# Layer 0 of a graph network: the products that place a quad's sums come two steps behind the sums, in two persistent PSUM tiles

## The chip, the cores and the metric

The kernel runs on one core of one Trainium2 chip. The metric is the device time of one execution in microseconds (us); less is better. The engines are TensorE (PE; PEld is its weight load), VectorE (DVE), ScalarE (ACT), GpSimd (POOL) and SyncE (SP), each with its own queue of instructions that it works off in order. PE can write only to PSUM, and DVE and ACT fetch its results from there.

## What is computed

Two layers over a graph of 3125 nodes with 128 features each and 100000 edges, which are sorted by their target node `dst`.

```python
# layer 0
summed = segment_sum(x[src], dst); deg = segment_sum(1, dst)
x = layernorm(x + elu((summed / maximum(deg, 1)) @ W + b))
# layer 1: attention per relation (4 relations, 4 heads of 128)
xl = einsum('nf,rfh->nrh', x, W_l); xr = einsum('nf,rfh->nrh', x, W_r)
z = leaky_relu(xl[src, type] + xr[dst, type] + e_feat)
score = einsum('ehc,ehc->eh', z, att[type]); alpha = softmax per (dst, type)
h_msg = gated mean over heads of segment_sum(alpha * xl[src, type])
h1 = layernorm(x + h_msg); h2 = layernorm(h1 + silu(h1 @ Wf1) @ Wf2)
x = layernorm(x + h2)
```

The change is in layer 0. Its sum over the edges of a node is what the steps below work out; while they run, the kernel also makes the tables xl and xr of layer 1 and turns the edges' attributes.

## The kernel before

The edges lie in 784 tiles of 128, four of which make a quad: 196 quads. The sums of layer 0 for all nodes are gathered in one accumulator in SBUF, acc0, that holds for each node 128 sums and its degree (repeated). The first 72 quads are handled by counting (`count`: for a block of nodes a matrix of counts is made and multiplied with the rows of x). The other 124 quads, u = 72 to 195, go through gathered rows, one quad in each step of a loop:

- `gather` (L768): POOL fetches the rows x[src] of a tile of 128 edges by an indirect DMA into a ring of 24 tiles, xg.
- `onehot4` (L1116): DVE makes for each of the quad's four tiles a one-hot matrix, edge by one of 32 neighbouring nodes.
- `sums0` (L1148): PE multiplies, so that the 32 sums of each tile come out, in the four quarters of a PSUM tile sg of 128 partitions x 129 columns (128 features and the count). After each of the four products the gather for the tile 24 further on is issued.
- `out_copy` (L1158): ACT copies sg to SBUF, sgs.
- `spread0` (L1162): DVE makes one more one-hot matrix, ohq, that says at which of 64 nodes each of the 4 x 32 sums belongs.
- `out0` (L1166): PE first makes six products whose result is used by nothing (il x ic, 300 columns of bf16 each, into columns 128 and up of the PSUM tile fo; called dummies below), and then the two products that place the quad's sums at their nodes, into columns 0 to 127 of fo.
- `add0` (L1176): DVE adds fo to acc0, at a column that it reads from a register.

All engines are handed their instructions through `Ordered` (L637), which keeps for each engine the order in which the program issues them; so the loop over the steps (L1360 to L1402) writes out by hand the order of every queue. The framework places the waits between the engines by the tiles that instructions read and write. PSUM has eight banks and all are in use: the pool l0p has one buffer each for mp, sg, fo and dn, the pool m0p one for mw and three for xp. l0 is a pool in SBUF, with two buffers of each tile where nothing else is said.

In step s the quad is u = 72 + s, and the order is: loads and stores on SP that are due; `out_copy(u-1)`; in steps that have edge work (each 2.3 steps or so), four transposes on PE of the edge attributes with ACT's copy emt (`turned`); halves of the table xr (DVE); `onehot4(u+1)` and `spread0(u)`; `out0(u-1)`; the edge work's products (`lin`); the counting matrices with `add0(u-1)` behind the first or instead of them; small jobs of a block; `sums0(u)`; a burst of products for the tables xl and xr of a block (`tables`, with ACT's copies xlr); and the stores of the edge work (`keep`: one of lb_d and four of eat_d on SP).

A block is 128 nodes whose sums are complete. `block(b, s)` (L1263) puts its phases into the steps from s on: it takes the sums, divides, multiplies with W, applies elu and layernorm, turns the result, and makes the block's part of the tables. L1352 says when it starts: when the last quad that has an edge to the block is behind (`behind`, L658), or at fixed steps for the first four.

```python
if u < NQ:
    spread0(u)
...
if UD < u <= NQ:
    out0(u - 1)
```

UD is 72 and NQ is 196.

Of the kernel before, what the change touches and what calls it, by code (L numbers as in the profile page):

```python
# [9 lines left out]
F32 = mybir.dt.float32  # L10
# [10 lines left out]
P = 128  # L21
N = 3125
E = 100000
F = 128
R = 4
H = 4
HC = H * F
# [594 lines left out]
WQ = 64  # L622
# [5 lines left out]
NQ = TT // 4  # L628
# [29 lines left out]
def behind(b):  # L658

    return min(NQ, -(-int(TT * (P * (b + 1) / N) ** 0.5 + 6) // 4))  # L660
# [5 lines left out]
UD, ND, SHI = 72, 240, NB2  # L666
# [26 lines left out]
def windows(ctx: ExitStack, tc: tile.TileContext, a, out, flag):  # L693
# [44 lines left out]
    def node(t, eng):  # L738
        return nc.values_load(d0_i[0:1, t:t + 1], engines=[eng], min_val=0, max_val=N - 1,
                              skip_runtime_bounds_check_because="a node's number")  # L740
# [16 lines left out]
    with tc.tile_pool(name="l0c", bufs=1) as l0c:  # L757
# [6 lines left out]
        ic = l0c.tile([P, 16 * SHI], BF16, name="ic")  # L764
        il = l0c.tile([P, P], BF16, name="il")
        pool = Ordered(tc, nc.gpsimd)

        def gather(t):  # L768
            pool.indirect_dma_start(out=xg[:, t % XG, :F], out_offset=None, in_=a["x"], in_offset=of_tile(t, src_e))


        with tc.tile_pool(name="pr", bufs=1) as pr, tc.tile_pool(name="prp", bufs=2, space=PSUM) as prp:
# [95 lines left out]
            b, k, f, l = (rm[:, :, o:o + P] for o in (0, P + 2, 2 * P + 2, 3 * P + 2))  # L868
# [15 lines left out]
        with tc.tile_pool(name="m0c", bufs=1) as m0c, tc.tile_pool(name="l0", bufs=2) as l0, \  # L884
# [3 lines left out]
            pe, ve, act, sp = (Ordered(tc, e) for e in (nc.tensor, nc.vector, nc.scalar, nc.sync))  # L888
# [224 lines left out]

            X = {}

            def onehot4(u):  # L1116
                o = X["oh", u] = l0.tile([P, 4, WA], F32, name="oh", bufs=3)
                ve.tensor_tensor(o, loc_e[:, 4 * u:4 * u + 4].unsqueeze(2).to_broadcast([P, 4, WA]),
                                 iw[:, :WA].unsqueeze(1).to_broadcast([P, 4, WA]), op=OP.is_equal)

            def turned(us):
                mp = bank()
                for j, u in enumerate(us):
                    c, i0 = u // QC, u * 4 % TR
                    pe.transpose(mp[:, j], ees[c][:, i0:i0 + 4].rearrange("p t s d -> p (t s d)"), ident)
                em = l0.tile([P, 4, P], F32R, name="emt", bufs=2)
                act.activation(em, mp, AF.Copy)
                X["emt", us[0]] = em

            def lin(us):  # L1130
                em = X["emt", us[0]].bitcast(F32)
                ln = X["ln"] = m0p.tile([P, 4, 4, H * R], F32, name="mw")
                for j in range(4):
                    pe.matmul(ln[:, j], em[:, j], vt, start=True, stop=True)

            def lin_add(us):
                lb = X["lb"] = l0.tile([P, 16, H, R], F32, name="lb")
                tng = others(4 * us[0])
                ve.tensor_tensor(lb, X.pop("ln").rearrange("p j t (h r) -> p (j t) h r", r=R),
                                 tng.unsqueeze(2).to_broadcast([P, 16, H, R]), op=OP.add)  # L1140

            def keep(us):
                sp.dma_start(lb_d[us[0] // 4], X.pop("lb").rearrange("p t h r -> p (t h r)"))
                em = X.pop(("emt", us[0])).bitcast(F32)
                for j, u in enumerate(us):
                    sp.dma_start(eat_d[u].rearrange("x (t e) -> t x e", t=4), em[:, j])

            def sums0(u):  # L1148
                o = X.pop(("oh", u))
                sg = l0p.tile([P, F + 1], F32, name="sg")  # L1150
                for i in range(4):
                    t = 4 * u + i
                    pe.matmul(sg[i * WA:(i + 1) * WA], o[:, i], xg[:, t % XG], start=True, stop=True)
                    if t + XG < TT:
                        gather(t + XG)
                X["sg", u] = sg

            def out_copy(u):  # L1158
                g = X["sgs", u] = l0.tile([P, F + 1], F32, name="sgs")
                act.activation(g, X.pop(("sg", u)), AF.Copy)  # L1160

            def spread0(u):  # L1162
                q = X["ohq", u] = l0.tile([P, WQ], F32, name="ohq")
                ve.tensor_scalar(q, iw[:, :WQ], rv[:, u:u + 1], None, op0=OP.is_equal)

            def out0(u):  # L1166
                g, q = X.pop(("sgs", u)), X.pop(("ohq", u))

                fb_ = l0p.tile([P, HC], F32, name="fo")
                for _ in range(6):  # L1170
                    pe.matmul(fb_[:, 2 * WQ:2 * WQ + 12 * SHI], il, ic[:, :12 * SHI], start=True, stop=True)
                fo = X["fo", u] = fb_[:, :2 * WQ].rearrange("p (a b) -> p a b", a=2)
                pe.matmul(fo[:, 0], g[:, :F], q, start=True, stop=True)
                pe.matmul(fo[:, 1], g[:, F:].to_broadcast([P, P]), q, start=True, stop=True)

            def add0(u):  # L1176
                n = node(4 * u, ENG.DVE)
                ve.tensor_tensor(acc0[:, :, ds(n, WQ)], acc0[:, :, ds(n, WQ)], X.pop(("fo", u)), op=OP.add)
# [18 lines left out]
            def count(u):  # L1197
                w = counted(u)
                cn = l0p.tile([P, SHI, w], F32, name="dn")
                for i in range(4):  # L1200
                    t = 4 * u + i
                    ol = l0.tile([P, P], BF16, name="ol", bufs=4)
                    ve.tensor_scalar(ol, il, lo_f[:, t:t + 1], None, op0=OP.is_equal)
                    oc = l0.tile([P, SHI * w], BF16, name="oc", bufs=4)
                    ve.tensor_scalar(oc, ic[:, :SHI * w], c_f[:, t:t + 1], None, op0=OP.is_equal)
                    pe.matmul(cn.rearrange("p a b -> p (a b)"), ol, oc, start=(i == 0), stop=(i == 3))
                X["cn", u] = cn

            def count_add(u):
                n = nc.values_load(dc_i[0:1, u:u + 1], engines=[ENG.DVE], min_val=0, max_val=ND - 1,  # L1210
                                   skip_runtime_bounds_check_because="a node's number, bounded")
                v = A[:, :, ds(n, counted(u))]
                ve.tensor_tensor(v, v, X.pop(("cn", u)), op=OP.add)
# [32 lines left out]
            C0, C2 = 3, []  # L1246
# [102 lines left out]
                    at_step(s + k[7] + 1, "half", lambda r=r: half(r))  # L1349

            for b in range(NB2):
                block(b, max(behind(b) - UD, C2[0] if b == 0 else C2[1] + 4 * (b - 1) if b < 4 else 0))  # L1352


            at_step(NS, "ve", rows_of_sources)
            for f in range(NQ // 4):
                at_step(turned_at(f), "edges", range(4 * f, 4 * f + 4))
            last = max(s for s, _ in jobs)
            onehot4(UD)
            for s in range(last + 1):  # L1360
                u = UD + s
                for f in jobs.pop((s, "sp"), []):
                    f()
                if UD < u <= NQ:
                    out_copy(u - 1)
                edges = jobs.pop((s, "edges"), [])
                for us in edges:
                    turned(us)
                halves_ = jobs.pop((s, "half"), [])
                if halves_:  # L1370
                    halves_.pop(0)()
                if u + 1 < NQ:
                    onehot4(u + 1)
                if halves_:
                    halves_.pop(0)()
                if u < NQ:
                    spread0(u)
                for f in halves_:
                    f()
                if UD < u <= NQ:  # L1380
                    out0(u - 1)
                for us in edges:
                    lin(us)
                counts = jobs.pop((s, "count"), [])
                for i, v in enumerate(counts):
                    count(v)
                    if i == 0 and UD < u <= NQ:
                        add0(u - 1)
                    count_add(v)
                if UD < u <= NQ and not counts:  # L1390
                    add0(u - 1)
                for us in edges:
                    lin_add(us)
                for e in ("act", "ve"):
                    for f in jobs.pop((s, e), []):
                        f()
                if u < NQ:
                    sums0(u)
                for f in jobs.pop((s, "burst"), []):
                    f()  # L1400
                for us in edges:
                    keep(us)  # L1402
# [5 lines left out]
    with tc.tile_pool(name="ac", bufs=1) as ac, tc.tile_pool(name="at", bufs=2) as at, \  # L1408
# [138 lines left out]
        pe, ve, act, pool, sp = (Ordered(tc, e) for e in (nc.tensor, nc.vector, nc.scalar, nc.gpsimd, nc.sync))  # L1547
# [270 lines left out]
        for s in range(-2, NQ + LATE + 2):  # L1818
            u = s - 1
# [37 lines left out]
    with tc.tile_pool(name="fc", bufs=1) as fc, tc.tile_pool(name="fw", bufs=3) as fw, \  # L1857
# [89 lines left out]
        for bs_ in QS:  # L1947
# [7 lines left out]
            b = bs_[0]  # L1955
# [28 lines left out]
```

## Time and profile before

| what | us |
|---|---|
| median of 5 runs | 2865.19 |
| lowest and highest of the 5 | 2854.01, 2869.36 |
| profiled execution | 2869.47 |
| its span, first to last instruction | 2867.6 |
| mean granted clock of TensorE over the span | 0.899 |
| layer 0's steps, in the span | 34.5 to 1077 |
| layer 1's loop, in the span | 1126 to 2786 |

The profile is of one execution. Times in a timeline count from the span's start. A row of a group gives engine, operation, out<-in with partitions x elements, and how many; behind the bar the busy time, the mean duration in ns, and the engine's idle time just ahead of these instructions with what ended it. In a timeline the bracket at a row's end is that idle time and its releaser. "remote" and "issue" are releases that the profile can't lay to an instruction of this core's engines. All of the helper's instructions have line L647, so one goes by the tiles' names. The granted clock is a share of full speed.

### The profile page before, as it was taken

How to read it: one execution, taken by the hardware profiler on the slowest of the kernel's cores; microseconds unless marked ns; L12 is line 12 of the kernel's file. 1: busy time of each engine (PE TensorE's matmuls, PEld its weight loads, DVE VectorE, ACT ScalarE, POOL GpSimd, SP SyncE). 2: the span in 40 equal slices, each digit the busy share in tenths (PEclk: the TensorE clock that was granted, in tenths of full speed). 3: DMA queues.
4: the chain of work that ended last, by engine and by line, in shares of the span. 5: the costliest groups of instructions: out<-in, count | busy, mean ns of one | idle time of the engine just before them, and what ended most of it. 6: DMA issues, size and time to landing. Idle time of an engine off the chain costs nothing.

```text
span 2867.6 us, 66163 instructions
## 1 busy us (share of the span) xinstructions
PE 2415.8 (84%) x24485; PEld 1859.7 (65%) x24485; DVE 1823.0 (64%) x6395; ACT 909.8 (32%) x1964; POOL 1245.2 (43%) x1294
## 2 busy tenths in 40 slices
PE   3677777877787785699999999999999999999964
PEld 2444454445444443477777777888888888888853
DVE  6655635653554345377777777777777777767656
ACT  0111112112222221244444444444444444333314
POOL 6544454344444413244444444444444444444400
PEclk9757778778788787799999999999999999999977
DMA  4323344334455456466666667777777789999920
GB/s 128 90 67 102 116 126 151 133 123 155 130 197 181 150 190 227 137 201 204 207 205 207 205 203 216 235 235 236 233 233 237 233 241 256 254 251 248 241 55 24
DMA packets 284394, 520.64 MB, mean 182 GB/s; under 512 B 45833, under 2 KB 144820, under 8 KB 283151
## 3 DMA queue, kind: packets, MB, share of 16 engines
q1 hardware_dynamic: 201588, 273.76, 30.6%
q0 software_dynamic: 78592, 239.71, 29.0%
q8 instruction: 194, 3.18, 0.5%
q10 hardware_dynamic: 3880, 2.84, 0.4%
q14 instruction: 140, 1.15, 0.1%
HBM read 412.10 MB, written 104.82 MB: 180 GB/s over the span
## 4 chain that ended last, share of the span: by engine, by line
PE 48%; DVE 8%; issue 3%; DMA 1%; ACT 0%; SPq 0%; DVEq 0%; ACTq 0%
PE z L647 30%; PE ag L647 7%; PE row L647 6%; DVE wo L647 4%; PE e L647 2%; PE sm_p L647 2%; DVE f L647 1%; DMA win<-xr_d 0%; DVE ea L647 0%; DVE oh L647 0%; PE f L1930 0%; PE f L1922 0%; DVE acc L647 0%; DVE y L647 0%; DMA xr_d<-xh 0%
## 5 line engine op out<-in xcount | busy, mean ns | idle before, releaser
L647 POOL DMA_INDIRECT xl<-xl_d,src_e x784 | 752.0, 959 | 890.0 <-PE ag L647 399.5
L647 POOL DMA_INDIRECT xg<-in_x_dram,src_e x496 | 488.7, 985 | 542.8 <-PE sg L647 366.3
L647 ACT ACTIVATE relu<-z 128x512 f32<-128x512 f32 x784 | 449.6, 597 | 796.3 <-PE z L647 619.5
L647 PE MATMUL z<-f_ident,xl 128*128 128x128 f32 x3136 | 476.5, 275 | 0.0
L647 PEld LDWEIGHTS z<-f_ident,xl 128*128 128x128 f32 x3136 | 369.0, 141 | 44.5 <-issue 0.8
L647 PE MATMUL z<-ea,weh 128*128 128x512 f32 x784 | 361.3, 461 | 18.1 <-issue 13.4
L647 PE MATMUL z<-oht,win 96*128 96x128 f32 (+2 forms) x1600 | 342.4, 297 | 2.2 <-DMA win<-xr_d 1.9
L647 PEld LDWEIGHTS z<-oht,win 128*128 128x128 f32 (+1 forms) x1600 | 275.3, 190 | 57.6 <-DMA win<-xr_d 2.1
L647 PE MATMUL z<-ea,wel 128*128 128x512 f32 x784 | 310.6, 396 | 0.0
L647 PE MATMUL row<-relu,attw 128*32 128x128 f32 x6272 | 246.6, 276 | 33.8 <-issue 31.2
L647 PE MATMUL ag<-xl,wo 128*32 128x128 f32 x6272 | 225.5, 278 | 7.5 <-DVE acc L647 4.2
L647 PEld LDWEIGHTS row<-relu,attw 128*32 128x32 f32 x6272 | 171.9, 109 | 88.6 <-issue 87.7
L647 DVE TENSOR_TENSOR acc<-acc,fo 128x128 f32 x124 | 35.4, 285 | 248.6 <-PE fo L647 76.5
L647 PEld LDWEIGHTS ag<-xl,wo 128*32 128x32 f32 x6272 | 180.7, 112 | 9.1 <-DVE acc L647 5.1
L647 DVE TENSOR_TENSOR_SCAN m<-rm,row 128x128 f32<-128x128 bf16 x98 | 41.3, 421 | 227.5 <-PE row L647 227.5
L647 PE MATMUL xp<-cbl,two 128*128 128x512 f32 x200 | 164.0, 820 | 24.4 <-DVE xh L647 12.7
L647 PE MATMUL fo<-ic,il 128*128 128x300 bf16 x744 | 154.0, 358 | 33.9 <-DVE acc L647 18.4
L647 PEld LDWEIGHTS z<-ea,weh 128*128 128x128 f32 x784 | 149.8, 191 | 27.4 <-issue 27.3
L647 DVE CAST xh<-xp 128x512 fp32r<-128x512 f32 x100 | 69.1, 691 | 145.7 <-PE xp L647 108.2
L647 PE MATMUL fo<-ohq,sgs 128*128 128x64 f32 x496 | 95.6, 329 | 73.3 <-issue 47.1
L647 PEld LDWEIGHTS z<-ea,wel 128*128 128x128 f32 x784 | 150.2, 192 | 8.6
L647 DVE SCALAR_TENSOR_TENSOR ea<-far,e 128x512 fp32r<-128x512 bf16 x196 | 132.3, 675 | 36.9 <-PE e L647 35.9
(327 smaller groups left out, 4034.1 us busy)
## 6 DMA issues: line engine op xcount, KB each, us to landing
win<-xr_d SPq DMA_DIRECT2D x224, 256.0 KB
xr_d<-xh SPq DMA_DIRECT2D x100, 512.0 KB
win<-xr_d SPq DMA_DIRECT2D x176, 192.0 KB
xl_d<-xlr SPq DMA_DIRECT2D x100, 258.0 KB
sg<-seg_d SPq DMA_DIRECT2D x196, 128.0 KB
rm<-rq_d SPq DMA_DIRECT2D x98, 128.5 KB
eat_d<-emt SPq DMA_DIRECT2D x196, 64.0 KB
xl<-xl_d,src_e POOLq DMA_INDIRECT x784
```

Of the source, the lines that this page charges most:

```text
L647: ins = f(*args, **kw)
```

## The change

Two PSUM tiles are made once, ahead of the loop, instead of a new tile each step: sgp with two halves of 129 columns, and fop with four parts of 128 columns. `sums0(u)` writes half u % 2 of sgp. `out0` is called for u-2 instead of u-1 and writes part u % 2 of fop; its dummies are seven of 256 columns, into parts 2 and 3 of fop, instead of six of 300. `add0` is called for u-2, too. sgs has three buffers instead of two, and ohq four instead of two. The blocks start one step later where their start depends on `behind` (from the fifth block on), so there are 129 steps instead of 128. `out_copy(u-1)`, `onehot4(u+1)`, `spread0(u)` and `sums0(u)` stay in their steps.

```diff
+            sgp = l0p.tile([P, 2, F + 1], F32, name="sg")
+            fop = l0p.tile([P, 4, P], F32, name="fo")
...
             def sums0(u):
                 o = X.pop(("oh", u))
-                sg = l0p.tile([P, F + 1], F32, name="sg")
+                sg = sgp[:, u % 2]
...
             def out_copy(u):
-                g = X["sgs", u] = l0.tile([P, F + 1], F32, name="sgs")
+                g = X["sgs", u] = l0.tile([P, F + 1], F32, name="sgs", bufs=3)
...
-                q = X["ohq", u] = l0.tile([P, WQ], F32, name="ohq")
+                q = X["ohq", u] = l0.tile([P, WQ], F32, name="ohq", bufs=4)
...
-                fb_ = l0p.tile([P, HC], F32, name="fo")
-                for _ in range(6):
-                    pe.matmul(fb_[:, 2 * WQ:2 * WQ + 12 * SHI], il, ic[:, :12 * SHI], start=True, stop=True)
-                fo = X["fo", u] = fb_[:, :2 * WQ].rearrange("p (a b) -> p a b", a=2)
+                for _ in range(7):
+                    pe.matmul(fop[:, 2:].rearrange("p a b -> p (a b)"), il, ic[:, :2 * P], start=True, stop=True)
+                fo = X["fo", u] = fop[:, u % 2].rearrange("p (a b) -> p a b", a=2)
...
-                block(b, max(behind(b) - UD, C2[0] if b == 0 else C2[1] + 4 * (b - 1) if b < 4 else 0))
+                block(b, max(behind(b) - UD + 1, C2[0] if b == 0 else C2[1] + 4 * (b - 1) if b < 4 else 0))
...
-                if UD < u <= NQ:
-                    out0(u - 1)
+                if UD + 1 < u <= NQ + 1:
+                    out0(u - 2)
...
-                    if i == 0 and UD < u <= NQ:
-                        add0(u - 1)
+                    if i == 0 and UD + 1 < u <= NQ + 1:
+                        add0(u - 2)
...
-                if UD < u <= NQ and not counts:
-                    add0(u - 1)
+                if UD + 1 < u <= NQ + 1 and not counts:
+                    add0(u - 2)
```

## Prediction

> **What bounds the kernel now.** I read the busy tenths first. TensorE is full for most of the second half, but in the first part, layer 0, it is not, and its clock changes.
>
> ```profile
> PE   3677777877787785699999999999999999999964
> PEclk9757778778788787799999999999999999999977
> ```
>
> Each digit is a slice of 71.7 us. The change touches slices 2 to 15 alone. The view of stretches, for the steps of layer 0 (34.5 to 1077 us; columns: stretch, length, busy time of PE, PEld, DVE, ACT, POOL, granted clock, DMA share, GB/s):
>
> ```profile
> 34.50:1077.00 1042.50, 787.81 (x4069) 495.13 (x4069) 522.55 (x1745) 214.70 (x509) 471.29 (x485) 0.80 0.42 136
> ```
>
> No engine is full: PE 76%, DVE 50%, POOL 45%, ACT 21%, DMA 42%. 124 steps in 1042.5 us are 8.4 us a step, so the stage is bound by hand-overs in the fixed order of issue; what is worth time is PE's idle time that nothing else would refill. The costliest groups give the stop that the change aims at:
>
> ```profile
> L647 PE MATMUL fo<-ic,il 128*128 128x300 bf16 x744 | 154.0, 358 | 33.9 <-DVE acc L647 18.4
> L647 PE MATMUL fo<-ohq,sgs 128*128 128x64 f32 x496 | 95.6, 329 | 73.3 <-issue 47.1
> ```
>
> PE stood still for 73.3 us just ahead of the placing products: that is the most that the lag can win by itself. Most of it is ended by "issue", which says nothing, so I read the timeline. PE's sums of quad 179 and what follows (columns: start, length, engine, operation, idle before and its releaser):
>
> ```profile
> 941.70 0.43 PE L647 MATMUL sg<-xg,oh 128*32 128x129 f32 x8
> ...
> 942.05 0.94 PE L647 MATMUL fo<-ic,il 128*128 128x300 bf16 x6
> ...
> 948.64 0.28 ACT L647 ACTIVATE sgs<-sg 128x129 f32<-128x129 f32 x1 [6.78 <-remote]
> ...
> 948.98 1.12 PE L647 MATMUL fo<-ohq,sgs 128*128 128x64 f32 x4 [5.98 <-issue]
> 949.78 0.55 PEld L647 LDWEIGHTS mw<-w,me 128*128 128x128 f32 x2
> 949.88 0.74 PE L647 MATMUL mw<-w,me 128*128 128x128 f32 x2
> ...
> 951.07 0.66 PE L647 MATMUL sg<-xg,oh 128*32 128x129 f32 x8
> ```
>
> The sums ended at 942.13, ACT copied them only at 948.64, and PE's placing products came 0.06 us after the copy's end (948.92). The releaser of ACT is not shown ("remote"); the copy was late, not slow (0.28 us).
>
> **The change, part by part.**
>
> *1. The placing products come from the quad before.* out0 now works on u-2, whose copy was issued a step earlier, so its stop at the copy goes. Through the timeline I sorted the 124 steps by the gap ahead of the placing products:
> - 81 steps have none: the six dummies take 0.94 us and the copy ends about 0.4 to 0.5 us after the sums. Gain 0; the dummies hide the copy.
> - 19 have a gap of 0.35 us or less, together 3.8 us, mostly 0.21 us after a burst of table products, whose copies stand ahead of this one on ACT. Gain 3.8.
> - 24 have more: 29.7 us in 10 "clear" steps, in which nothing else stops PE before the next sums, and 39.7 us in 14 "blocked" ones.
>
> Then I asked what is late next. sums0(u) writes the tile that out_copy(u-1) reads, as before. The new tile has two halves of 129 columns (1032 bytes per partition in all), and the halves would free PE entirely only if each had its own guard. The trace has one tile that several engines share by parts, hm, with four parts of 128 columns:
>
> ```profile
> 2786.24 2.82 PE L1902 MATMUL hm<-f_ident,acc 128*128 128x128 f32 x12 [0.32 <-DVE acc L647]
> 2787.40 0.50 DVE L1886 BATCH_NORM_STATS2 fst<-hm 128x6 f32<-128x128 f32 x2 [1.21 <-PE hm L1902]
> ...
> 2790.90 1.58 ACT L1905 ACTIVATE fr<-hm 128x512 f32<-128x512 f32 x3 [5.71 <-DVE fmv L1887]
> ```
>
> DVE read the first part only after the fourth was written (the first transpose of a tile ended at 2786.72, the fourth at 2787.36), and ACT's read waited until DVE's reads were over. So I take such a tile to be guarded whole: sums0(u) still waits for out_copy(u-1), and PE wins in a clear step only the work between the placing products and the next sums. Behind that stop stand, on PE, the sums, a burst of tables and the next dummies, and on POOL the gathers for quad u+6, which are issued behind the sums; all of them stood behind the old stop too. For quad 179 that is 951.07 - 948.98 = 2.09 of 5.98 us. Summed over the ten clear steps, the smaller of gap and such work is 15.2 us (quad 75: 2.46 of 5.48; 73: 1.79 of 4.05; 159: 1.05 of 6.27; 179: 2.09; 149: 1.86; 142: 1.61; 117: 1.56; 154: 1.37; 100: 0.83; 99: 0.61).
>
> The Trainium skill, "PSUM — Partial Sum Buffer", section "PSUM bank collisions raise a hardware error ⚠️", says the same from the other side: PSUM is to be guarded by bank and quadrant, not by address, because two engines in one bank collide even on different columns. By that rule the two halves of a 2 KiB bank buy no overlap between PE's sums and ACT's copy, and this part is worth the sum just given; without it the sum would be that of rival B.
>
> *Blocked steps.* There the next product needs another late thing. Quad 164:
>
> ```profile
> 809.14 1.11 PE L647 MATMUL fo<-ohq,sgs 128*128 128x64 f32 x4 [4.08 <-issue]
> ...
> 812.29 0.60 ACT L647 ACTIVATE emt<-mp 128x512 fp32r<-128x512 f32 x1 [3.19 <-remote]
> ...
> 812.94 1.97 PE L647 MATMUL mw<-vt,emt 128*128 128x64 f32 x8 [2.68 <-issue]
> ```
>
> If PE places 4.08 us earlier, it stops for ACT's emt at the same 812.94. In twelve of the fourteen the next stop is such a one (ACT's emt, or DVE's ol and oc ahead of the counts): gain 0. In two (184 and 188) a transpose can start early, so that ACT's ht and what hangs on it follow; I take 2.2 + 1.8 = 4.0 us.
>
> *2. The dummies.* Seven products of 256 columns are 1792 columns instead of 1800. Six take 0.94 us in the rows above, so seven at 256 cost about the same; they still wait for DVE's add of the step before (the wait behind 18.4 us of the row above), since they write the tile that it reads. 124 more pairs of weight load and product: 0, with 0 to 5 us as bounds (0.04 us each, if the load were not hidden).
>
> *3. More buffers* (sgs 3, ohq 4): no instruction, no DMA. add0, onehot4 and spread0 keep their places; add0 in step u adds what out0 made in the same step, as before. 0. In the stage DVE is idle for some 247 us ahead of the adds, some 75 of it for these products, but they come earlier only where PE does, so it is not counted again.
>
> *4. Blocks start a step later, and the steps are 129.* From the schedule I counted which jobs fall into the same step: table bursts with edge steps 10, then 7; halves with edges 8, then 7; means with edges 8, then 9; bursts with two-count steps 1, then 3. All DMAs of a block (its input rows, ht, xl and xr tables) move one step on SP with it; SP and the queues move 136 GB/s here and layer 1 moves over 200 in the same profile, so I give this 0, with -8 to +12 us as bounds: about one step either way.
>
> At the end, quad 195 was placed between 1075.68 and 1077.3 (dummies, 0.93; placing, 0.55; add, 0.29). Now the last step has one more round of dummies and placing behind an add, while the earlier rounds move ahead of the last burst: +0.5 to +2.5; I take +1.5.
>
> **Sum:** -3.8 - 15.2 - 4.0 + 1.5 = -21.5. The profiled execution took 2869.5 us (span 2867.6), so 2848 for a like one. It is 4.3 above the median of the runs shown, 2865.2; against that I forecast **2844**.
>
> **The rivals.**
>
> *B, the halves are guarded each by itself.* Then the clear steps win their whole 29.7 us, the small ones 3.8, and the dummies lose the 18.4 us wait for DVE's add: -52, 2813. For it: the code asks for halves. Against it: the rows of hm. 0.1.
>
> *C, nothing is won.* ACT's copy is late for a cause outside the stop. In long gaps SP is busy storing eat_d, and all of ACT, DVE and POOL show "remote" releases, as at 808.81 and 812.29. If such a delay strikes the work after the sums just as well, the 15.2 and 4.0 us come back as stops of PE ahead of sums0 or lin, and only the 3.8 is left: 2861. For it: twelve of fourteen blocked steps refill their gap already. Against it: the ten clear ones do not. Within 0.3% either way. 0.25.
>
> *D, slower, by the clock.* PE's busy time in the stage is 787.8 us at a granted clock of 0.80, and slices of it stand between 0.5 and 0.8. Whoever moves idle time from one place to another moves the stretches at a lower clock too. If the stage came out at 0.78 instead of 0.80, its busy time would be 787.8 x 0.80/0.78 = 808: +20, and if no stop of the 15.2 us is won with it, the time is 2865 + 20 - 3.8 = 2881. It decides from a loss of 0.02 on, where it eats the whole gain. For it: a PE that waits before the sums instead of between dummies and placing has its dummies, which are there to keep it busy, in another place. Against it: total idle falls. With it goes a bad placing of the shifted blocks (+12). 0.2.
>
> **How the numbers follow.** Forecast 0.45, B 0.1, C 0.25, D 0.2. About 0.3% (8.6 us) is what a measurement of this kernel can tell from no change. Faster: all of the forecast and B make 0.55. Same: C, 0.25. Slower: D, 0.2. The forecast's own range, with the 0 to 5 of the dummies and -8 to +12 of the shift, is 2836 to 2861. The range for 8 in 10 takes in C, the greater part of B's side and the lower part of D's: 2815 to 2878.
>
> **What would show it.** In the profile after: the idle ahead of the placing products falls from 73.3 us to under 10; the idle ahead of sg<-xg,oh rises by about 30 to 50, ended by ACT's sgs (if B holds, it does not, and PE does the sums of one quad while ACT copies the other); the dummies' wait for DVE's acc stays near 18; ACT's sgs rows keep their long "remote" waits; the stage ends some 20 us earlier, about 1056, at a clock of 0.80 or a little above. A stage clock below 0.79 means D. A stage as long as before, with the idle time only moved ahead of sg, means C. Layer 1 must stay as it is: if its length of 1660 us (1126 to 2786) moves by over 5 us, I have missed something.

## The result, and the profile after

The changed kernel is slower: 2883.56 us (median of 52 runs, 2867.48 to 2906.81) against 2869.21 us for the kernel before (94 runs, 2854.01 to 2893.91). The ratio is 1.0044, 95% interval 1.0033 to 1.0055, that is +12.6 us (+9.5 to +15.8) of 2869.2. Forecast was 2844, -21 us.

The profiled execution took 2870.9 us (span 2869.2) and is one of the faster ones of this kernel, so the two profiles lie only 1.5 us apart; the loss has to be read by stages and from the experiments. First the page's tenths, then the view of stretches for layer 0's steps (same columns as before), which now end at 1088 instead of 1077:

```profile
PE   2686766778787785599999999999999999999964
PEclk9667777887788787799999999999999999999977
```

```profile
34.50:1088.00 1053.50, 778.25 (x4193) 505.40 (x4193) 526.60 (x1749) 212.27 (x507) 472.96 (x485) 0.77 0.41 135
```

The steps take 11 us longer although PE is busy for 9.6 us less: PE's idle time grew. The groups of that stretch show where it went (columns: busy time, mean ns | idle time just ahead, its releasers):

```profile
L647 PE MATMUL fo<-ic,il 128*128 128x256 bf16 x868 | 153.0, 332 | 33.6 <-DVE acc L647 25.0 <-issue 8.4
L647 PE MATMUL fo<-ohq,sgs 128*128 128x64 f32 x496 | 84.8, 304 | 0.0
L647 PE MATMUL mw<-vt,emt 128*128 128x64 f32 x392 | 69.3, 335 | 61.1 <-issue 35.8 <-ACT emt L647 25.3
L647 PE MATMUL sg<-xg,oh 128*32 128x129 f32 x992 | 67.2, 353 | 28.5 <-issue 16.5 <-DVE oh L647 9.5 <-ACT sgs L647 2.5
```

The stop ahead of the placing products is gone, all 73.3 us of it. In the kernel before, the same view gives for the other two groups:

```profile
L647 PE MATMUL mw<-vt,emt 128*128 128x64 f32 x392 | 71.0, 341 | 25.8 <-issue 21.5 <-ACT emt L647 4.2
L647 PE MATMUL sg<-xg,oh 128*32 128x129 f32 x992 | 66.8, 351 | 9.3 <-DMA xf<-in_L_gnn_W_e_dram 9.3
```

So 35 us came back ahead of the edge work's products, which wait for ACT's emt, and 19 ahead of the sums; the counting products took 20 more (their idle time with that of their weight loads went from 37.8 to 57.3 us in the union of PE's records). PE's whole idle time from the first sums to the last placing, from that union of products and weight loads, is 273.5 us instead of 253.3.

One place of the changed kernel's timeline shows how (some of POOL's gathers are left in):

```profile
784.79 0.66 PE L647 MATMUL sg<-xg,oh 128*32 128x129 f32 x8
...
785.38 1.12 PE L647 MATMUL mp<-f_ident,ee 128*128 128x128 f32 x4
...
786.07 0.95 POOL L647 DMA_INDIRECT xg<-in_x_dram,src_e  x1 [0.30 <-issue]
...
786.29 1.70 PE L647 MATMUL fo<-ic,il 128*128 128x256 bf16 x7
...
787.32 0.95 POOL L647 DMA_INDIRECT xg<-in_x_dram,src_e  x1 [0.30 <-issue]
...
787.78 0.80 PE L647 MATMUL fo<-ohq,sgs 128*128 128x64 f32 x4
788.58 0.95 POOL L647 DMA_INDIRECT xg<-in_x_dram,src_e  x1 [0.30 <-issue]
790.01 0.28 ACT L647 ACTIVATE sgs<-sg 128x129 f32<-128x129 f32 x1 [6.50 <-PE fo L647]
790.18 0.94 POOL L647 DMA_INDIRECT xg<-in_x_dram,src_e  x1 [0.66 <-PE fo L647]
792.76 0.60 ACT L647 ACTIVATE emt<-mp 128x512 fp32r<-128x512 f32 x1 [2.48 <-remote]
792.88 0.29 DVE L647 TENSOR_TENSOR acc<-acc,fo 128x128 f32 x1 [5.85 <-remote]
...
793.41 1.97 PE L647 MATMUL mw<-vt,emt 128*128 128x64 f32 x8 [4.83 <-ACT emt L647]
```

PE ended the sums at 785.45, the transposes at 786.50 and the placing products at 788.58. ACT could copy the sums only at 790.01 (4.56 us late), the transposes at 792.76, and DVE could add only at 792.88 (4.30 us late), each with nothing else to do (that the first of these rows names PE's fo is the view's guess at which of PE's signals came; the copy needs the sums). PE did not stop ahead of fo, as meant, and stood at the next thing that needs ACT. All the while POOL issued one gather after the other.

### The profile page after: what moved, and what is told of

Read it like the earlier page. It is cut to its first block, busy times and chain, and to the rows that moved or that the text cites. A ratio compares the mean times of both kernels' runs of the same rounds, so it can differ in the third digit from the quotient of the medians.

```text
span 2869.2 us, 66382 instructions
## 1 busy us (share of the span) xinstructions
PE 2402.6 (84%) x24609; PEld 1866.1 (65%) x24609; DVE 1826.2 (64%) x6395; ACT 906.1 (32%) x1962; POOL 1247.0 (43%) x1294
## 4 chain that ended last, share of the span: by engine, by line
PE 48%; DVE 8%; issue 3%; DMA 1%; ACT 0%; SPq 0%; DVEq 0%; ACTq 0%
PE z L647 30%; PE ag L647 7%; PE row L647 6%; DVE wo L647 4%; PE e L647 2%; PE sm_p L647 2%; DVE f L647 0%; DMA win<-xr_d 0%; DVE ea L647 0%; DVE oh L647 0%; PE f L1932 0%; PE f L1924 0%; DVE acc L647 0%; DMA xr_d<-xh 0%; DVE fst L1888 0%
## 5 line engine op out<-in xcount | busy, mean ns | idle before, releaser
L647 DVE TENSOR_TENSOR_SCAN m<-rm,row 128x128 f32<-128x128 bf16 x98 | 41.2, 421 | 222.6 <-PE row L647 220.3
L647 PE MATMUL fo<-ic,il 128*128 128x256 bf16 x868 | 153.0, 332 | 33.6 <-DVE acc L647 25.0
L647 PE MATMUL xp<-cbl,two 128*128 128x512 f32 x200 | 167.6, 838 | 15.8 <-DVE xh L647 6.8
L647 ACT ACTIVATE xlr<-xp 128x512 f32<-128x512 f32 x100 | 59.7, 597 | 306.1 <-PE xp L647 163.1
```

The lines of the kernel that those rows point to most:

```text
L647: ins = f(*args, **kw)
```

## The experiments

Each ratio is to the kernel before, run on the same chip in the same set; the kernel's own medians differ by 1% between sets (2865.7 to 2895.8), so times are compared within a set. Ratios shift a little between sets, too: e7 and n7 are the same kernel and gave 0.9108 and 0.9080.

| run | what | ratio to before, 95% interval |
|---|---|---|
| e1_shift | blocks one step later, nothing else | 1.0041 (1.0023 to 1.0059) |
| e2_tiles | persistent tiles, 7 dummies, no lag, no shift | 1.0000 (0.9981 to 1.0018) |
| e3_lag_old_tiles | lag and shift, old tiles | 1.0052 (1.0025 to 1.0080) |
| e4_lag_no_shift | lag and tiles, blocks as before | 0.9986 (0.9964 to 1.0008) |
| e5_shift_to_19 | blocks 4 to 19 later | 1.0055 (1.0030 to 1.0081) |
| e6_shift_from_20 | blocks 20 to 24 later | 1.0028 (1.0008 to 1.0049) |
| e7_before_no_refill | no gathers in the steps | 0.9108 (0.9075 to 0.9141) |
| e8_lag_no_refill | lag, no gathers | 0.9098 (0.9062 to 0.9133) |
| e9_two_xp | two xp (yardstick) | 1.0192 (1.0157 to 1.0227) |
| e10_lag_two_banks | lag, two banks for sg, two xp | 1.0216 (1.0178 to 1.0253) |
| e11_plain_loads | SP's plain loads for the gathers | 0.9193 (0.9157 to 0.9228) |
| e13_edges_too | blocks 1 to 24 and edge work later | 1.0074 (1.0045 to 1.0104) |
| n7_no_refill | as e7, yardstick | 0.9080 (0.9043 to 0.9117) |
| n1_shift_no_refill | shift, no gathers | 0.9120 (0.9079 to 0.9162) |
| n5_to_19_no_refill | blocks 4 to 19 later, no gathers | 0.9114 (0.9076 to 0.9153) |
| n6_from_20_no_refill | blocks 20 to 24 later, no gathers | 0.9071 (0.9034 to 0.9108) |
| n14_all_later_no_refill | all 25 blocks later, no gathers | 0.9128 (0.9097 to 0.9159) |
| m1_lag_all_later | the change, with blocks 0 to 3 later too | 1.0016 (0.9997 to 1.0035) |

**Which part of the change costs.** Three theories: the later blocks, the dummies and tiles, or the lag itself. Four kernels take the parts singly.

```diff
 e1:  block(b, max(behind(b) - UD + 1, ...))            on the kernel before
 e2:  sgp, fop and 7 dummies of 256                     on the kernel before
 e3:  sg, fo and 6 dummies of 300 as before             on the changed kernel
 e4:  block(b, max(behind(b) - UD, ...))                on the changed kernel
```

> The kernel before with nothing but the blocks' start one step later (from the fifth block on, 129 steps). If the loss of 12 to 14 us is the later blocks (their last phases end one step of about 8.4 us later, and their jobs fall on other edge steps), this alone gives +8 to +14 us. If the lag or the dummies make the loss, it is within 4 us of the kernel before.

> The kernel before with the two persistent PSUM tiles and seven dummies of 256 columns, but without the lag and without the shift: out0 and add0 stay at u-1. If the loss is the dummies (one more weight load and product a step, or a wait that the shared tile adds), this gives +8 to +14 us; if it is the lag or the shift, 0 within 4.

> The lag of two steps and the shift of the blocks with the tiles of before: a new sg and fo each step, six dummies of 300 columns. If the dummies or the shared tiles make the loss, this is no slower than before (0 to -20 us, as the prediction had it). If the lag or the shift makes it, the loss of 12 to 14 us stays.

> The changed kernel, but the blocks start in the steps of before; so a block that starts right behind its last quad takes the sums without that quad's share, and its values leave that share out. If the later blocks make the loss, this is level with the kernel before or faster (-8 to 0). If the lag or the dummies make it, +8 to +14 us stays.

The later blocks alone make +0.41%, as much as the whole change (+0.44%). Tiles and dummies make nothing that can be measured (0 within 5.4 us). With the lag but without the later blocks the kernel is level with before, -0.14% (-0.36 to +0.08). And e3 against e1 says the same of the lag: 0.52 against 0.41. So two steps of the prediction failed: the lag, priced at 21.5 us, wins nothing that can be measured, and the shift, put at 0, costs about 12.

**Why the lag wins nothing.** The theory: PE's signals reach ACT and DVE late while POOL issues gathers, and PE, once it no longer stops for the first late signal, stops for the next. The rivals: the whole guard of the shared tile eats the gain (the prediction's own step), or the signals are late for a cause other than POOL.

```diff
 e7, e8:                     if t + XG < TT:
-                        gather(t + XG)
 e11:
-                        gather(t + XG)
+                        r0 = (t + XG) * 37 % (N - P)
+                        sp.dma_start(xg[:, t % XG, :F], a["x"][r0:r0 + P, :])
```

> The kernel before, but no gathers in the steps: the ring of 24 tiles is filled once and its rows are used again, so that the sums of the later quads are of other rows. If PE's signals reach ACT and DVE late because POOL is issuing gathers, the waits marked remote ahead of sgs (136 us) and acc (76 us) nearly vanish and layer 0 shortens by 60 to 150 us. If the signals are late for another cause (SP's stores, PE itself), they stay, and layer 0 shortens by less than 30 us.

> The kernel with the lag and the tiles of the change, the blocks in the steps of before, and no gathers in the steps (as in the run beside it; the blocks at the end take their sums without the last quad). If the late signals ate what the lag wins, the lag now shows its gain against the same kernel without it: 8 to 20 us less. If the stop is hidden anyway once the signals are in time, both are equal within 5 us.

> The kernel before, with the refill of the ring made by plain loads of 128 neighbouring rows that SP issues, in place of POOL's gathers: the same bytes arrive, of other rows. If PE's signals are late because POOL issues gathers, the time falls nearly as far as without any refill (below 2680 us). If it is the traffic into SBUF that makes them late, it stays above 2800 us.

Without the gathers the kernel takes 2610.1 us (2606.9 to 2612.2) beside 2865.7: 256 us less, more than expected. The steps end at 817 us instead of 1077. The view of stretches and the groups of e7:

```profile
34.50:818.00 783.50, 672.86 (x4070) 432.87 (x4071) 517.42 (x1750) 214.73 (x509) 18.46 (x13) 0.91 0.41 142
```

```profile
L647 PE MATMUL fo<-ohq,sgs 128*128 128x64 f32 x496 | 77.9, 284 | 9.5 <-ACT sgs L647 9.3 <-issue 0.2
L647 DVE TENSOR_TENSOR acc<-acc,fo 128x128 f32 x124 | 35.3, 284 | 81.1 <-PE fo L647 73.8 <-remote 6.5
L647 ACT ACTIVATE sgs<-sg 128x129 f32<-128x129 f32 x124 | 34.7, 280 | 174.1 <-PE sg L647 169.9 <-remote 3.8
```

Against the kernel before, in the same view:

```profile
L647 DVE TENSOR_TENSOR acc<-acc,fo 128x128 f32 x123 | 35.1, 285 | 247.2 <-remote 76.4 <-PE fo L647 75.1 <-PE mw L647 31.2
L647 ACT ACTIVATE sgs<-sg 128x129 f32<-128x129 f32 x124 | 34.8, 281 | 302.0 <-PE sg L647 143.7 <-remote 136.3 <-PE mp L647 18.6
```

DVE and ACT are as busy as before, but "remote" falls from 136.3 to 3.8 us ahead of sgs and from 76.4 to 6.5 ahead of the adds, and the stop ahead of fo from 73.3 to 9.5. Counted over the 124 copies, the start lies over 0.5 us behind both the sums' end and ACT's work before in 35 copies of the kernel before (112 us together), 35 of the changed one (122 us), and 1 without gathers (4 us). In the kernel before, 3 of the 68 copies were late whose sums began when POOL was through with every gather due, and 32 of the other 56.

It is PE's signals that are late, not ACT or DVE. In the semaphore events of the trace of the kernel before, at quad 150, eight signals of PE whose instructions ended between 680.36 and 683.59 us are all recorded between 689.15 and 689.47; DVE starts its add at 689.17 and ACT its copy at 689.49. Over the steps 391 of the 1084 recorded signals of PE come over 0.1 us behind the last end of an instruction that gives one (237 more are not recorded); without gathers 8 of 948. The other way nothing is late: in both kernels PE starts none of 124 placing products, 123 rounds of dummies and 49 of edge products over 0.06 us behind the end of ACT's or DVE's work that they wait for, or of PE's own. Nor does PE wait for the gathered rows: its 9.3 us ahead of the sums are the start of the loop.

With plain loads from SP in place of the gathers, as many bytes arrive and 2 copies are late; the time, 2664.0 us of a kernel at 2893.9 in that set, is nearly as low as without any. So it isn't the amount that is moved; it goes with POOL's gathers. These loads fetch neighbouring rows, so that it is the issuing and not the scattered rows is argued from the 3 of 68 against 32 of 56 above and not shown by a run of its own. By what path on the chip a gather holds PE's signals back, no run here shows.

Without gathers the lag gives 2605.5 against 2610.1 us of the same set. The ranges of the four runs each overlap (2599.0 to 2610.5 and 2606.9 to 2612.2), so these 4.6 us are not clear of noise. From the first sums to the last the profiled executions take 774.6 us instead of 779.7, but n7, the same kernel as e7, takes 782.5. With punctual signals the dummies cover the copy in nearly every step (17 of 124 have a gap, one of them 6.2 us), so of the stop only 9.5 us are left to win. The 8 to 20 us of the expectation were not there.

Then the guard of the shared tile. One bank of PSUM is freed by taking a buffer of xp, which has its own price, so the yardstick pays it too:

```diff
 e9, e10:
-                        xp, xq = (m0p.tile([P, HC], F32, name="xp", bufs=3) for _ in range(2))
+                        xp, xq = (m0p.tile([P, HC], F32, name="xp", bufs=2) for _ in range(2))
 e10 (on e4):
-                sg = sgp[:, u % 2]
+                sg = l0p.tile([P, F + 1], F32, name="sg", bufs=2)
```

> The kernel before with two buffers of xp instead of three, which frees a PSUM bank and is only the yardstick for the run beside it. The tables' bursts lose a buffer, so it is slower than before, by 10 to 60 us.

> The lag without the later blocks, with two banks for sg instead of two halves of one (and two buffers of xp, as in the yardstick beside it; the blocks at the end take their sums without the last quad). If the whole guard of the shared tile ate what the lag should win (the prediction's step, rival B's price of 52 us against 21.5), this is 20 to 50 us below the yardstick. If PE only meets the next late signal, it is within 10 us of it.

With two banks the time is 2951.0 us against 2945.0 of the yardstick, within 10 us. The groups of the steps, first of the yardstick, then of the kernel with two banks:

```profile
L647 PE MATMUL fo<-ic,il 128*128 128x300 bf16 x744 | 153.1, 357 | 28.6 <-DVE acc L647 26.5 <-issue 2.0
L647 PE MATMUL fo<-ohq,sgs 128*128 128x64 f32 x496 | 94.5, 326 | 79.5 <-issue 54.3 <-ACT sgs L647 25.2
L647 PE MATMUL mw<-vt,emt 128*128 128x64 f32 x392 | 70.6, 339 | 27.9 <-issue 21.5 <-ACT emt L647 6.5
```

```profile
L647 PE MATMUL fo<-ic,il 128*128 128x256 bf16 x868 | 150.8, 328 | 57.5 <-DVE acc L647 55.7 <-issue 1.7
L647 PE MATMUL fo<-ohq,sgs 128*128 128x64 f32 x496 | 86.5, 309 | 0.0
L647 PE MATMUL mw<-vt,emt 128*128 128x64 f32 x392 | 71.0, 340 | 70.9 <-issue 49.9 <-ACT emt L647 20.8
L647 PE MATMUL sg<-xg,oh 128*32 128x129 f32 x992 | 65.4, 343 | 10.5 <-DMA xf<-in_L_gnn_W_e_dram 9.6 <-issue 0.9
```

Now PE stops neither ahead of fo nor ahead of the sums (10.5 us is the start of the loop), and the 79.5 us stand elsewhere: +43 ahead of the edge products (emt) and +29 ahead of the dummies (DVE's add of the step before, whose own signal from PE is late). The guard is real: in the changed kernel no quad's sums begin before the copy of the quad before has ended, with two banks those of 8 quads do. But it isn't what ate the gain.

What ate it can be read step by step. Of the prediction's ten clear steps the five with the longest gaps (quads 73, 75, 149, 159 and 179) are together 28.2 us shorter in e10 than in the yardstick, from the start of the quad's sums to the start of the next ones; to the start of the sums after those they are 2.4 us longer. In e4, beside e2, the same five are 8.1 us shorter, where the prediction had 9.25, and over two steps 1.1 us. (Before and e2, both without the lag, differ by 1.3 us in that sum and by up to 3.4 in one step, so the 28.2 are clear of it and the 8.1 less so.) The lag does win in the clear step, and a step later it is gone.

**What the later blocks cost.** First theory: how the moved blocks fall on the other jobs, or the end of the layer. e5 and e6 part the blocks, and e13 moves the edge work along.

```diff
 e5:  block(b, max(behind(b) - UD + (b < 20), ...))
 e6:  block(b, max(behind(b) - UD + (b >= 20), ...))
 e13: block(b, max(behind(b) - UD, ...) + (b > 0));  turned_at: return 7 + f * (NS - 11) // (NQ // 4)
```

> The kernel before, with the blocks 4 to 19 alone one step later (no lag, old tiles). If the loss of the shift comes from how the jobs of the many blocks fall on edge steps and on the fixed blocks 1 to 3 (the tables of block 16 now fall into the step of those of block 3), this alone gives +8 to +14 us. If it comes from the last five blocks, which stand nearest to the end, it gives 0 within 4.

> The kernel before, with the last five blocks (20 to 24) alone one step later. If the loss of the shift comes from the end (the tables of block 22 now stand between the last sums and their placing, and blocks 23 and 24 begin a step later), this gives +8 to +14 us; by the other theory 0 within 4.

> The kernel before with all blocks but the first one step later, the fixed blocks 1 to 3 too, and the edge work one step later with them, so that they meet each other as before. If the 12 us of the shift come from which jobs fall into one step, most of it goes: -3 to +6 us against the kernel before. If a later start costs by itself, the +12 us stays.

Both parts cost, as neither expectation had it: blocks 4 to 19 +0.55%, the last five +0.28%. They don't add up to the 0.41% of both, and the intervals are wide. For the last five the trace shows a place: from the last sums to layer 1's first product pass 52.5 us in the kernel before (1075.4 to 1127.9) and 65.0 in e6 (1072.3 to 1137.3), because the tables of block 22 now follow the last sums; the steps ahead are shorter by only a part of it. This lengthening is in all nine kernels whose last five blocks come later, the change among them (64 to 65 us, against 51 to 54 in the other eleven). Moving the edge work along did not help, it was worse (+0.74%): that theory, as put, falls. Block 0 stayed in its step there, so the tables of block 9 still met those of block 0.

Without gathers the runs of a kernel scatter over 3 to 12 us only, so the same question was put there.

> The kernel before without the refill of the ring (the sums of the later quads are of other rows), once more, as the yardstick of the three runs beside it: 0.911 of the kernel before, as it was (0.9075 to 0.9141).

> All blocks from the fifth on one step later, without the refill of the ring (the sums of the later quads are of other rows). If the later blocks cost by themselves, by the end or by what shares a step, the 12 us stay against the yardstick: +8 to +14. If they cost only by where they meet the gathers, 0 within 4.

> Blocks 4 to 19 alone one step later, without the refill of the ring (the sums of the later quads are of other rows). If the middle blocks cost by which jobs share a step, +6 to +14 us against the yardstick; if they cost only beside the gathers, 0 within 4.

> The last five blocks alone one step later, without the refill of the ring (the sums of the later quads are of other rows). If the end costs by itself (a burst of tables more behind the last sums, which the steps before them don't give back), +4 to +10 us against the yardstick; if not, 0 within 3.

In one set: yardstick 2624.2 us (2619.0 to 2625.5), all from the fifth on 2637.2 (2629.3 to 2640.6), blocks 4 to 19 alone 2635.7 (2631.4 to 2637.5), the last five alone 2622.3 (2622.0 to 2625.2). So the loss of +13 us doesn't need the gathers, and without them it sits in the middle blocks alone: from the last sums to layer 1's first product n6 takes 12.5 us more as well, but from the first sums to the last 11.1 us less. Traces of one kernel repeat to 0.1 us in most steps (90 of 123 between e7 and n7). A moved block mostly takes its time from one step to the next; in two places more is added, worked out from the starts of the sums (us from one quad's sums to the next):

| step | 61 | 62 | 63 | sum | | 99 | 100 | 101 | sum |
|---|---|---|---|---|---|---|---|---|---|
| yardstick | 3.8 | 16.0 (tables 9) | 13.7 (tables 0) | 33.5 | | 3.8 | 11.3 (tables 16) | 12.2 (tables 3) | 27.3 |
| blocks 4 to 19 later | 5.6 | 9.9 | 25.7 (tables 0 and 9) | 41.2 | | 6.8 | 2.9 | 25.6 (tables 3 and 16) | 35.3 |

Where the tables of a moved block fall into the step of a fixed one (blocks 0 to 3 start at fixed steps), the step's own work no longer lies beside two bursts but beside one. That was the next theory, and two last kernels took the collisions away by moving all 25 blocks.

```diff
 n14, m1: block(b, max(behind(b) - UD, ...) + 1)
```

> All 25 blocks one step later, the fixed ones 0 to 3 too, without the refill of the ring (the sums of the later quads are of other rows). If the loss of 12 to 13 us is the two steps that take the tables of two blocks (9 with 0, 16 with 3), it goes: within 4 us of the kernel without refill, 0.908 to 0.910 of the kernel before. If a later start costs anyhow, 0.912 as with the blocks 4 to 24 moved.

> The changed kernel with the fixed blocks 0 to 3 one step later too, so that no step takes the tables of two blocks but the last. If the two shared steps make the change's loss, this is level with the kernel before, -4 to +5 us (the lag's 0 to -4 and the end's few). If they don't, +8 to +14 us as the change.

They don't settle it. In the change, moving the fixed blocks too gave 1.0016 (0.9997 to 1.0035) instead of 1.0044 (1.0033 to 1.0055): most of the loss away, if ratios of two sets may be compared so closely. Without gathers no step but the last holds two bursts, and the loss stays, at 0.9128 (2639.8 us); but the set had no yardstick of its own, and against the two of other sets it is 0.0020 or 0.0048, where it was 0.0040 with the fixed blocks in place. In the traces n14 (its step s+1 beside n7's s, which hold the same blocks' jobs) is 6 to 9 us behind in most of steps 20 to 50 and 13 to 19 us from step 99 on, gathered a little here and there. To the last placing PE's idle time is 9.7 us longer and its busy time 6.3; beside e7's trace, another execution of n7's kernel, it is 4.4 and 14.4, so this parting says little. So this stays open: that the blocks' later start costs is measured in both settings, the collisions are seen in the traces, but whether they are the whole cause isn't shown, and what the rest would be wasn't settled.

## Why the prediction was wrong

- *What bounds the kernel.* Right that no engine is full and that the steps are bound by hand-overs. Wrong that a hand-over taken away is worth the work until the next one: the wait's cause was a late signal, and it strikes every hand-over from PE. "The copy was late, not slow" was read off the timeline, and that its release was marked remote was noted; but rival C looked to SP's stores, and the six gathers that POOL issued from 941.88 to 948.82 us were not considered.
- *Step 1, the stop goes.* Right: 73.3 us to 0.0.
- *Step 1, clear and blocked steps (-15.2 and -4.0).* This step failed. It followed PE up to the next sums and booked what was won by then as time of the kernel. The places were right, and not of one execution: the copies of nine of the ten clear steps are late in e2 and in e4 as well. But the gain is gone one step later (8.1 us in the five largest, 1.1 over two steps), because the next products of PE that need ACT or DVE meet the late signals: 35 us came back ahead of the edge products, 19 ahead of the sums. Measured, the lag is worth -0.14% (-0.36 to +0.08). Rival C's mechanism, a delay that strikes the work after as well, was the right one for the lag, though not its price of -3.8 us, which nothing here can tell from 0.
- *The guard.* Right that sums0 still waits: PE stands for the copy in 8 steps, 19.0 us together (a rise of 30 to 50 was expected). Wrong that this decides. Without the guard (two banks) nothing more is won, so rival B was wrong at its price, too. That the kernel guards the shared tile whole agrees with the rule in the Trainium skill, "PSUM — Partial Sum Buffer", section "PSUM bank collisions raise a hardware error ⚠️", to guard by bank and quadrant and not by address; it had no bearing on the time.
- *Step 2, dummies, and step 3, buffers: 0.* The dummies with the tiles: right, 1.0000 (0.9981 to 1.0018). The buffers were not run alone; e4, which has them with the lag, is level.
- *Step 4, the later blocks.* This is the step that set the sign: put at 0 with -8 to +12 us as bounds, it measures +0.41% (+0.23 to +0.59), some 12 us. Coincidences of edge steps were counted; that two steps would hold the tables of two blocks could be read from the same schedule, and so could the tables behind the last sums. How much of the 12 us each of them makes stays open.
- *Rival D, the clock.* Slower it became, and the clock of the steps is 0.77, under D's sign of 0.79; but D's price was 20 us more of busy PE, and PE is busy for 9.6 us less. e2 has 0.77, too, at no loss. What D took in beside the clock, a bad placing of the shifted blocks at +12, is what came.
- *Layer 1 stays.* Its stretch from the first product to the end differs by up to 10 us between executions of kernels in which it is the same (1648 to 1658 us from its first edge product to the final stage, in the profiles of before, after and e1 to e6), so the check on 5 us was too sharp.

## What to carry to other kernels

When waits are long, many and marked as released from outside, find what makes the signal late before pricing the wait: what is won up to the next stop may be paid there, so count it over the steps behind, too. A change that needs the schedule moved by a step has two prices, and the schedule's is best measured alone, first: here it was all of the loss. And where signals are late, the schedule decides which: of the 35 late copies before, 31 are late in e2 and in e4 again, whose blocks keep their steps, but 21 in e1 and in the change, whose blocks don't.

## What the runs showed of the hardware that was not expected

PE's signals are late while POOL issues indirect gathers. Taking away the 472 gathers of the steps (0.95 us busy, 1.25 us apart when in a row) made the kernel 256 us shorter; with plain loads from SP in their place it was 230 us shorter. With gathers 35 of 124 copies on ACT started 0.6 to 7.2 us late, without them one, with the plain loads two. PE itself is also faster there: its granted clock in the steps is 0.91 instead of 0.80, and its busy time 673 instead of 788 us for the same products, so about 115 of the 256 us are busy time and the rest is idle time. This points to the gathers, not the placing, as what layer 0's time hangs on.
